# Keeping all sixteen pieces of image 0 on chip between its statistics and its first convolution

## The chip, the cores and the metric

The kernel runs on one core of a Trainium2 chip. The metric is device time in microseconds (us); lower is better. Engines are called PE (TensorE), DVE (VectorE), ACT (ScalarE), POOL (GpSimd) and SP (SyncE, which here only issues DMAs). Three runs of the kernel before gave a median of 11134.48 us (11132.05 to 11135.5).

## What is computed

The input x is four images of 192 channels and 128x128 pixels, f32. Two layers, both of the form x = x + conv(group_norm(x)):

```
x = x + L0(_gn(x))      # layer 0: 1x1 conv 192 -> 48 channels, split in three groups of 16:
                        #   x_0 : 1x1 conv
                        #   x_05: fractional Fourier transform in 2-D, magnitude and phase,
                        #         3x3 conv inside a window and 1x1 convs on them, transform back
                        #   x_1 : real 2-D FFT, 1x1 convs on magnitude and phase, inverse FFT
                        #   concatenate, 1x1 conv 48 -> 192
x = x + L1(_gn(x))      # layer 1: layer norm, projection, causal conv, selective scan over
                        #   16384 tokens with 384 channels x 16 states, gate, projection
_gn: 32 groups of 6 channels, mean and variance over a group's channels and all pixels
```

The change is in layer 0's group norm and its first 1x1 convolution, both of image 0. The group norm needs the mean and variance over the whole image before the first pixel can be convolved, so the image is read twice: once for the statistics, once for the convolution.

## The kernel before, in words

Layer 0 (`layer0`, L122) handles an image in sixteen pieces of 8 rows (1024 pixels); a piece is a tile of 96 partitions x 2 x 1024 f32, 768 KB, 8 KB of each partition. It has four generators for an image:

- `analysis` (L266): loads each piece (`load`, L196, a DMA issued by SP at L199), takes its statistics (`bn`, L202: four BATCH_NORM_STATS2 on DVE, L205), then combines them (L218, then the small matmuls L56 and L63 and the DVE steps L57 to L67 of `_group_stats`), scales the weights (L284), forms a bias (L287, L291) and convolves each piece: four matmuls (L301), one eviction with the bias on ACT (L305) into `x1`, and after each pair of pieces two DMAs of 192 KB, issued by ACT (L311), to the DRAM tensor `d1`. `x1` has two buffers (pool `l0f`), each for one pair.
- `forward` (L314): loads 32 of the 48 channels of `d1` as one image `img` (2 MB, L317 on SP), transforms (`spectrum`, matmuls L233 and L243, evictions L236 and L249 on ACT, L251 on DVE) and forms magnitude and phase (`_polar`, L70: eleven steps on DVE, a RECIPROCAL of 6.54 us among them, L84 to L96). This goes in three passes: two halves of the fractional transform, then the real FFT. Results go to DRAM (`dmag` and `dp` at L326, `dh` at L333). The pool `l0u` with seven buffers holds a pass.
- `backward` (L337): convolutions on magnitude and phase, and the transforms back.
- `synthesis` (L481): last convolution, added to x, written to `xmid`, and the statistics for layer 1.

The sixteen pieces' tiles come from the pool `l0x` of seven buffers, which `analysis` and `synthesis` of all images share. The last four pieces (KEEP = 4) stay on chip between the statistics and the convolution; the convolution takes these first and then the other twelve, which are loaded a second time from x.

`weave` (L520) calls the generators of up to four images in turn: first `analysis` of image 0 alone, then in step p `backward` of image p-1, `forward` of p, `analysis` of p+1 and `synthesis` of p-2. This sets the order in which the program is written. In layer 0 the compiler then orders the instructions of each engine itself, by its own estimate of when each is ready and by their place in the program, and adds the waits. The order on an engine or a DMA queue is fixed from then on: an instruction that waits holds up all behind it on its engine. Layer 1 (`layer1`, L593) has an order written out by hand, which the change doesn't touch; it takes over when layer 0's pools are closed, and its scans run from 1377 us to the end.

Of the kernel before, what the change touches and what calls it, by code (L numbers as in the profile page):

```python
# [33 lines left out]
NPIECE = S // ROWS  # L34
# [87 lines left out]
def layer0(tc, x, xmid, st2, w):  # L122

    nc = tc.nc
    B = x.shape[0]
    KEEP = 4
    LOADS = 14
    with ExitStack() as ctx, ExitStack() as inner:
        def pool(name, bufs, ctx=inner, **kw):
            return ctx.enter_context(tc.tile_pool(name=name, bufs=bufs, **kw))  # L130

        kp = pool("l0k", 1, ctx)
        dram = pool("l0d", B, ctx, space=DRAM)
        xp = pool("l0x", 7, ctx)
        sp = pool("l0s", 2, ctx)
        psB = pool("l0r", 2, ctx, space=PSUM)
        cp = pool("l0c", 1)
        fp = pool("l0f", 2)
        imp = pool("l0i", 2)
        zp = pool("l0z", 2)  # L140
        up = pool("l0u", 7)
        vp = pool("l0v", 4)
        qp = pool("l0q", 1)
        psA = pool("l0p", 4, space=PSUM)

        def const(name, cp=cp):
# [46 lines left out]
        def split(v):  # L193
            return v.rearrange("(t p) f -> p t f", p=CH)

        def load(b, p):  # L196
            xt = xp.tile([CH, 2, PIECE], F32, name="xt")
            src = x[b].rearrange("c h w -> c (h w)")[:, p * PIECE : (p + 1) * PIECE]
            nc.sync.dma_start(out=xt, in_=split(src))  # L199
            return xt  # L200

        def bn(st, p, xt):  # L202
            for t in range(2):
                for q in range(PIECE // 512):
                    nc.vector.bn_stats(  # L205
                        st[:, t, p * (PIECE // 512) + q, :], xt[:, t, q * 512 : (q + 1) * 512]
                    )
# [7 lines left out]
        def bn_done(st, out, psum):  # L215
            mv = sp.tile([CH, 2, 2], F32, name="mv")
            for t in range(2):
                nc.vector.bn_aggr(mv[:, t, :], st[:, t, :, :])  # L218
            _group_stats(nc, sp, psum, g_ones, mv, out, 1e-5)
# [43 lines left out]
            nc.tensor.matmul(ps[:, 0:n], bd[:, i, :], rhs, start=True, stop=True)  # L263
            return ps[:, 0:n]

        def analysis(b, got):  # L266


            st = sp.tile([CH, 2, NPIECE * (PIECE // 512), 6], F32, name="st")
            kept = {}  # L270
            for p in range(NPIECE):
                xt = load(b, p)
                if p >= NPIECE - KEEP:
                    kept[p] = xt
                bn(st, p, xt)
                yield
            gst = sp.tile([CH, 2, 2], F32, name="gst")
            bn_done(st, gst, in_a)

            w1r = fp.tile([CH, 2, 128], F32, name="w1r")
            for t in range(2):
                nc.vector.tensor_scalar(w1r[:, t, :], w1T[:, t, :], gst[:, t, 1:2], None, ALU.mult)  # L284
            ps = psA.tile([128, 512], F32, name="ps")
            for t in range(2):
                nc.tensor.matmul(  # L287
                    ps[:, 0:1], w1r[:, t, :], gst[:, t, 0:1], start=t == 0, stop=t == 1
                )
            b1 = fp.tile([128, 1], F32, name="b1")  # L290
            nc.vector.tensor_scalar(b1, ps[:, 0:1], -1.0, None, ALU.mult)  # L291
            d1 = got["d1"] = dram.tile([3 * NC, S * S], F32, name="d1")
            for p in (*range(NPIECE - KEEP, NPIECE), *range(NPIECE - KEEP)):
                xt = kept.pop(p, None) or load(b, p)
                if p % 2 == 0:
                    x1 = fp.tile([128, 2, 512], F32, name="x1")
                ps = psA.tile([128, 512], F32, name="ps")
                for t in range(2):
                    for q in range(2):
                        half = slice(64 * q, 64 * (q + 1))  # L300
                        nc.tensor.matmul(  # L301
                            ps[half], w1r[:, t, half], xt[:, t, q * 512 : (q + 1) * 512],
                            start=t == 0, stop=t == 1,
                        )
                nc.scalar.activation(x1[:, p % 2, :], ps, AF.Identity, bias=b1)  # L305
                if p % 2 == 1:
                    at = d1[:, (p - 1) * PIECE : (p + 1) * PIECE].rearrange(
                        "c (e q f) -> q c e f", e=2, q=2
                    )
                    for q in range(2):  # L310
                        nc.scalar.dma_start(out=at[q], in_=x1[64 * q : 64 * q + 3 * NC])  # L311
                yield
# [168 lines left out]
        def synthesis(b, got, early):  # L481
# [5 lines left out]
            def fetch(p):  # L487
                if p < NPIECE:
                    cat = cats[p % 2]
                    for q in range(2):  # L490
                        at = slice(p * PIECE + q * 512, p * PIECE + (q + 1) * 512)
                        nc.sync.dma_start(out=cat[64 * q : 64 * q + NC, :], in_=d1[0:NC, at])
                        nc.sync.dma_start(out=cat[64 * q + NC : 64 * q + 3 * NC, :], in_=dimg[:, at])
                if len(early) <= p + len(early) < NPIECE:
                    xts.append(load(b, p + len(early)))
# [24 lines left out]
        def weave(works, early=None):  # L520

            n = max(count for _, count in works)
            for i in range(n):
                for work, count in works:
                    for _ in range((i + 1) * count // n - i * count // n):
                        next(work, None)
                if early is not None and i == LOADS:
                    early.extend(load(B - 1, p) for p in range(KEEP))
            for work, _ in works:
                for _ in work:  # L530
                    pass

        got = [{} for _ in range(B)]
        weave([(analysis(0, got[0]), 1)])
        early = []
        for p in range(B + 1):
            works = []
            if p:  # L540
                works.append((backward(p - 1, got[p - 1]), 19))
            if p < B:
                works.append((forward(p, got[p]), 9))
            if p + 1 < B:
                works.append((analysis(p + 1, got[p + 1]), 2 * NPIECE + 1))
            if p >= 2:
                works.append((synthesis(p - 2, got[p - 2], []), NPIECE + 1))
            weave(works, early if p == B else None)
# [697 lines left out]
def program(tc, x, out, w):  # L1246
    B = x.shape[0]
    with (
        tc.tile_pool(name="keep", bufs=1) as keep,
        tc.tile_pool(name="mid", bufs=1, space=DRAM) as mid,  # L1250
    ):
        st2 = keep.tile([CH, B, 2, 2], F32, name="st2")
        xmid = [mid.tile([C, S * S], F32, name=f"xmid{b}") for b in range(B)]
        first = layer0(tc, x, xmid, st2, w)
        second = layer1(tc, xmid, [out[b].rearrange("c h w -> c (h w)") for b in range(B)], st2, w)
        next(first)
        next(second)
        ready = False
        for _ in first:
            for _ in range(2):  # L1260
                ready = ready or next(second)
        for _ in second:
            pass
# [16 lines left out]
```

## Time and profile before

| | before |
|---|---|
| median of three runs | 11134.48 us |
| the profiled execution's own time | 11134.09 us |
| its span, first to last instruction | 11132.3 us |
| loads of pieces in layer 0 (`xt<-in_x`, 768 KB each) | 176 |
| image 0: last statistics on a piece end | 68.4 us |
| image 0: first and last convolution eviction start | 79.65 and 118.53 us |
| `img` of image 0: load issued, first transform matmul | 127.52 and 137.76 us |
| image 1: statistics combined (L218) | 191.59 us |
| image 1: first and last matmul of its first convolution | 208.0 and 261.7 us |
| `img` of image 1, 2, 3: load issued | 269.80, 521.47, 795.92 us |
| layer 1's scans begin | 1377 us |

How to read it: times of instructions are in us from the span's start. A line of a timeline gives the start, the duration, the engine, the line of the code, the operation, the tiles (out<-in) and how many instructions were merged; in square brackets the idle time of the engine before it and what ended that. SPq and ACTq are the DMA queues that SP and ACT issue from. In a table of stretches, the columns give busy time (and number) of each engine, the granted TensorE clock as a share of full speed, the mean busy share of the 16 DMA engines and what they moved. The span and the execution's own time differ by 1.8 us, which lie around the span.

### The profile page before, as it was taken

The numbers are of one execution on the slowest core, as the hardware profiler recorded it, in microseconds if no ns is written. First come the engines' busy times: TensorE is split into PE (matmuls) and PEld (weight loads), VectorE is DVE, ScalarE is ACT, GpSimd is POOL, SyncE is SP. The second block draws the span as 40 slices with busy tenths as digits, with TensorE's granted clock in tenths as the row PEclk, the third lists the DMA queues.
The fourth block names the chain that finished last, engine by engine and source line by source line (L and its number), as shares of the span: only waits on it lengthen the run. The fifth ranks groups of instructions, "written<-read, shape, count | busy, mean of one in ns | idle before, by whom it ended". The sixth has DMA issues, their size and how long they took to land.

```text
span 11132.3 us, 168105 instructions
## 1 busy us (share of the span) xinstructions
PE 9935.4 (89%) x55026; PEld 6973.1 (63%) x55026; DVE 10209.6 (92%) x11587; ACT 9346.5 (84%) x19303; POOL 9523.9 (86%) x4342
## 2 busy tenths in 40 slices
PE   4777799999999999999999999999999999999998
PEld 2444366666666666666666666666666666666666
DVE  5666699999999999999999999999999999999999
ACT  2333299999999999999999999999999999999997
POOL 0000199999999999999999999999999999999999
PEclk8888799999999999999999999999999999999999
DMA  8786734434434434434334334344444334344343
GB/s 235 187 228 177 234 106 118 123 103 121 123 107 119 117 108 124 114 110 125 114 110 125 113 112 124 111 113 125 113 111 125 113 110 124 108 117 123 108 118 96
DMA packets 1357308, 1416.61 MB, mean 127 GB/s; under 512 B 920730, under 2 KB 972175, under 8 KB 1355791
## 3 DMA queue, kind: packets, MB, share of 16 engines
q1 hardware_dynamic: 1335950, 1342.94, 43.4%
q0 software_dynamic: 13312, 50.34, 1.4%
q10 hardware_dynamic: 7168, 12.59, 0.3%
q8 instruction: 436, 7.14, 0.3%
q14 instruction: 442, 3.61, 0.1%
HBM read 1230.12 MB, written 155.33 MB: 124 GB/s over the span
## 4 chain that ended last, share of the span: by engine, by line
PE 46%; ACT 23%; DVE 15%; issue 5%; DMA 2%; POOL 0%; SPq 0%; DVEq 0%; POOLq 0%; ACTq 0%
PE ps L1014 12%; PE ps L798 12%; DVE h L988 10%; ACT da L910 8%; PE op L974 7%; PE ps L1053 6%; ACT L695 4%; DVE op L931 3%; ACT op L910 3%; ACT dbT L959 2%; PE ps L951 1%; ACT L810 1%; ACT u L810 1%; PE ps L767 1%; DMA carry<-h 1%
## 5 line engine op out<-in xcount | busy, mean ns | idle before, releaser
L1001 POOL TENSOR_TENSOR hc<-h,c 128x1024 f32<-128x1024 f32 x3072 | 7220.9, 2369 | 326.3 <-DVE h L988 174.3
L988 DVE TENSOR_TENSOR_SCAN h<-da,carry,op 128x512 f32<-128x512 f32 x4464 | 5526.6, 1262 | 137.9 <-DMA carry<-h 134.5
L910 ACT ACTIVATE da<-dt,c_A_log 128x512 f32<-128x512 f32 x4608 | 3251.1, 737 | 239.6 <-DVE h L988 221.4
L1014 PE MATMUL ps<-ident,hc 128*128 128x128 f32 x24576 | 3315.0, 281 | 4.5 <-POOL hc L1001 4.5
L1014 PEld LDWEIGHTS ps<-ident,hc 128*128 128x128 f32 x24576 | 2943.8, 147 | 344.7 <-issue 312.5
L959 ACT ACTIVATE dbT<-ps,bT 128x128 f32<-128x128 f32 x8192 | 2274.6, 397 | 0.0
L798 PE MATMUL ps<-s,wc 128*128 128x512 f32 x4608 | 2129.8, 593 | 0.0
L974 PE MATMUL op<-ident,dbT 128*128 128x128 f32 x8192 | 1456.4, 300 | 628.8 <-ACT dbT L959 478.1
L988 DVE TENSOR_TENSOR_SCAN h<-op,carry,db 128x512 f32<-128x512 f32 x1488 | 1837.6, 1262 | 2.0 <-ACT da L910 1.1
L942 POOL TENSOR_TENSOR db<-dtu,b 128x1024 f32<-128x1024 f32 x768 | 1820.8, 2371 | 6.1 <-DVE nmr L641 6.1
L974 PEld LDWEIGHTS op<-ident,dbT 128*128 128x128 f32 x8192 | 1037.7, 149 | 1144.8 <-ACT dbT L959 534.8
L931 DVE TENSOR_TENSOR op<-ps,b 128x512 f32<-128x512 f32 x2560 | 1719.1, 672 | 3.9 <-ACT ps L891 3.9
L798 PEld LDWEIGHTS ps<-s,wc 128*128 128x128 f32 x4608 | 804.9, 190 | 682.8 <-issue 682.3
L910 ACT ACTIVATE op<-dt,c_A_log 128x512 f32<-128x512 f32 x1536 | 1084.2, 706 | 167.4 <-DVE h L988 166.5
L1053 PE MATMUL ps<-yg,c_woT 128*96 128x512 f32 x1536 | 702.7, 594 | 0.0
L695 ACT ACT_TABLE_LOAD x511 | 655.6, 1283 | 9.7 <-PEq L1270 0.7
L514 POOL DMA_DIRECT2D xmid<-xt x64 | 42.3, 661 | 569.9 <-DVE xt L510 542.6
L856 POOL TENSOR_TENSOR dtu<-dt,u 128x512 f32<-128x512 f32 x384 | 490.8, 1278 | 0.6 <-DMA cat<-dimg 0.6
L817 ACT ACTIVATE zs<-ps 128x512 f32<-128x512 f32 x384 | 229.4, 597 | 304.6 <-PE ps L805 304.6
L1053 PEld LDWEIGHTS ps<-yg,c_woT 128*96 128x96 f32 x1536 | 244.0, 163 | 338.4 <-issue 338.4
L205 DVE BATCH_NORM_STATS2 st<-xt 96x6 f32<-96x512 f32 x512 | 322.4, 677 | 100.5 <-DMA xt<-in_x 99.3
L78 POOL TENSOR_TENSOR u<-u 128x1024 f32<-128x1024 f32 (+1 forms) x12 | 29.7, 2477 | 447.6 <-ACT u L77 447.6
(173 smaller groups left out, 10018.9 us busy)
## 6 DMA issues: line engine op xcount, KB each, us to landing
c<-dbc SPq DMA_DIRECT2D x1024, 512.0 KB, 4.7
b<-dbc SPq DMA_DIRECT2D x768, 512.0 KB, 4.7
xt<-in_x SPq DMA_DIRECT2D x176, 768.0 KB, 8.3
xmid<-xt POOLq DMA_DIRECT2D x64, 768.0 KB, 6.3
xm<-xmid SPq DMA_DIRECT2D x128, 384.0 KB, 3.7
carry<-h SPq DMA_DIRECT2D x3072, 1.0 KB, 1.9
xr<-xmid SPq DMA_DIRECT2D x128, 384.0 KB, 6.1
out<-xr SPq DMA_DIRECT2D x128, 384.0 KB, 3.3
```

Source lines behind the costliest of these rows:

```text
L695: nc.scalar.preload_act_table_set("natural_log_exp_and_others")
L798: nc.tensor.matmul(g["c", j][0], wc[:, j, k, :], rhs, start=k == 0, stop=k == 5)
L856: nc.gpsimd.tensor_tensor(g["dtu", j], g["dt", j], g["u", j], ALU.mult)
L910: nc.scalar.activation(da, got[n]["dt", j], AF.Exp, scale=A[:, j, st : st + 1])
L931: nc.vector.tensor_tensor(dbs[s], g["dp", j][0], g["b", k % NG][:, q, :], ALU.mult)
L942: nc.gpsimd.tensor_tensor(db, _bc(g["dtu", j], 1, G), g["b", sg], ALU.mult)
L959: nc.scalar.activation(t[:, blk, :], g["tu", j][0][:, at], AF.Identity, scale=g["bT"][:, blk, st : st + 1],)
L974: nc.tensor.transpose(db[:, blk * 128 : (blk + 1) * 128], t[:, blk, :], ident)
L988: nc.vector.tensor_tensor_scan(h[:, q, :], das.pop(s), dbs.pop(s) if db is None else db[:, q, :], 0.0 if ch == 0 else g["before"][:, j, st ...
L1001: nc.gpsimd.tensor_tensor(hc, h, g["c", sg], ALU.mult)
L1014: nc.tensor.matmul(py[:, blk, :], hc[:, q, blk * 128 : (blk + 1) * 128], ident, start=first, stop=sg == NG - 1 and q == G - 1 and blk == N ...
L1053: nc.tensor.matmul(g["po", t][0][0:CH], woT[:, j, t * CH : (t + 1) * CH], g["yg", j], start=j == 0, stop=j == NJ - 1,)
```

## The change

For image 0 alone, `analysis` keeps all sixteen pieces. Pieces 0 to 8 go to a new pool `l0y` of nine buffers (72 KB of each partition), pieces 9 to 15 to the seven buffers of `l0x`. The convolution takes pieces 10 to 15 first, then 0 to 9, and loads none again. The new pool is closed as soon as this `analysis` has been written; the five pools `l0i`, `l0z`, `l0u`, `l0v` and `l0q` of the later steps (107,008 bytes of each partition by their tiles' sizes), which used to be opened at the start, are opened after it at the address at which the new pool stood. The other images keep KEEP = 4 and load twelve pieces again.

```diff
     KEEP = 4
+    XBUFS = 7
     LOADS = 14
...
-        xp = pool("l0x", 7, ctx)
+        xp = pool("l0x", XBUFS, ctx)
...
         fp = pool("l0f", 2)
-        imp = pool("l0i", 2)
-        zp = pool("l0z", 2)
-        up = pool("l0u", 7)
-        vp = pool("l0v", 4)
-        qp = pool("l0q", 1)
         psA = pool("l0p", 4, space=PSUM)
...
-        def load(b, p):
+        def load(b, p, xp=xp):
...
-        def analysis(b, got):
+        def analysis(b, got, more=None):
...
             kept = {}
+            keep = NPIECE if more else KEEP
             for p in range(NPIECE):
-                xt = load(b, p)
-                if p >= NPIECE - KEEP:
+                xt = load(b, p, more if more and p < NPIECE - XBUFS else xp)
+                if p >= NPIECE - keep:
                     kept[p] = xt
...
-            for p in (*range(NPIECE - KEEP, NPIECE), *range(NPIECE - KEEP)):
+            last = NPIECE - (XBUFS // 2 * 2 if more else KEEP)
+            for p in (*range(last, NPIECE), *range(last)):
                 xt = kept.pop(p, None) or load(b, p)
...
         got = [{} for _ in range(B)]
-        weave([(analysis(0, got[0]), 1)])
+        with tc.tile_pool(name="l0y", bufs=NPIECE - XBUFS) as more:
+            weave([(analysis(0, got[0], more), 1)])
+        imp = pool("l0i", 2)
+        zp = pool("l0z", 2)
+        up = pool("l0u", 7)
+        vp = pool("l0v", 4)
+        qp = pool("l0q", 1)
         early = []
```

## The prediction

> **What bounds the kernel now.** I read the page's slices first, to see where the change can act at all.
>
> ```profile
> ## 2 busy tenths in 40 slices
> PE   4777799999999999999999999999999999999998
> PEld 2444366666666666666666666666666666666666
> DVE  5666699999999999999999999999999999999999
> ```
>
> A slice is 278 us. Layer 0 fills the first five, and no engine is full there; from the sixth on layer 1's scans keep DVE, PE and POOL full. The table of stretches gives the same in numbers.
>
> ```profile
> 270.00:1377.00 1107.00, 820.98 (x2952) 451.19 (x2952) 722.47 (x905) 323.58 (x461) 95.91 (x111) 0.84 0.77 208
> 1377.00:11132.00 9755.00, 8988.85 (x51589) 6460.64 (x51588) 9348.12 (x10476) 8963.65 (x18762) 9420.66 (x4224) 0.96 0.41 115
> ```
>
> The columns are PE, PE's weight loads, DVE, ACT, POOL, clock, DMA share, GB/s. From 270 to 1377 us PE is busy 74%, DVE 65%, DMA 77%: layer 0 is bound by chains of waits in fixed orders, not by an engine. Layer 1's 9755 us are DVE at 96% and are not touched. So a gain can only be a layer 0 that ends earlier. The chain of waits that ended last breaks off at 898 us, so it says nothing on the start; I read timelines there. SP:
>
> ```profile
> 79.64 39.16 SPq L199 DMA_DIRECT2D xt<-in_x  x13
> 127.52 0.81 SPq L317 DMA_DIRECT2D img<-d  x1
> 128.39 8.08 SPq L199 DMA_DIRECT2D xt<-in_x  x7
> ```
>
> 32 loads of pieces stand ahead of img: 16 for image 0's statistics, 12 reloads, 4 of image 1. Three reloads were issued before 79.64; the 13 seen here are nine reloads and four loads of image 1. ACT, which evicts the convolution:
>
> ```profile
> 107.85 1.27 ACT L305 ACTIVATE x<-ps,b 128x512 f32<-128x512 f32 x2 [6.20 <-DMA d<-x]
> ...
> 118.53 1.27 ACT L305 ACTIVATE x<-ps,b 128x512 f32<-128x512 f32 x2 [6.79 <-DMA d<-x]
> ```
>
> It waits 25.3 us in all, six times, for the write of d1 that holds its x1 buffer, while PE's own waits for a reload are 4.6 us. The image's convolution is paced by writes that share the DMA engines with loads (0.99 busy from 82 to 127.5 us), not by the reloads' arrival as such. Then image 1, on DVE and PE:
>
> ```profile
> 116.57 2.47 DVE L205 BATCH_NORM_STATS2 st<-xt 96x6 f32<-96x512 f32 x4 [40.37 <-DMA xt<-in_x]
> ```
>
> ```profile
> 193.62 0.45 PE L56 MATMUL ps<-mv,c_g_ones 96*96 96x2 f32 x2 [30.38 <-DVE mv L218]
> 203.19 0.45 PE L63 MATMUL ps<-gs_d,c_g_ones 96*96 96x2 f32 x2 [9.11 <-DVE gs_d L61]
> 207.52 0.56 PE L287 MATMUL ps<-gst,w1r 96*128 96x1 f32 x2 [3.88 <-DVE w1r L284]
> ```
>
> ```profile
> 137.70:191.60 53.90, 24.37 (x96) 20.02 (x96) 48.19 (x65) 19.36 (x25) 4.71 (x2) 0.72 0.96 235
> ```
>
> DVE is idle 40 us for want of image 1's pieces, then from 137.7 to 191.6 it is 89% busy, because 12 pieces' statistics (48 instructions, 29.7 us) fall between the polar steps of forward of image 0. PE stands 43.4 us at the head of its queue for image 1's statistics. This is where the time is.
>
> **What the Trainium skill says.** "DMA: Bandwidth & Descriptors", section "Issuing engines are not separate DMA queues": DMAs from ACT and SP run on the same 16 engines and interleave. The trace agrees: a 192 KB write of d1 beside loads lands after 7.9 us (median). The same page, "Anatomy of one DMA — SWDGE (gpsimd) path": a wait happens on the issuing sequencer before dispatch, so it holds all behind it; SP's L326 waited 20.4 us for ACT with eight loads of pieces behind it. "TensorE: Matmul & The Clock Gate", Part 1: PE idles down to half clock after some microseconds; the trace grants 0.50 from 110 to 140 us, where PE waits. No page prices the reuse of a closed pool's memory.
>
> **The change part by part.** Sum against the profiled execution, 11134.1 us (span 11132.3, 1.8 around it; the median is 0.4 higher).
>
> 1. *First sixteen loads.* They need no freed buffer now. Statistics start every 3.155 us (24.88 to 65.90 us in 13 gaps) of which DVE works 2.47: DMA sets the pace with 1.02 to 1.04 busy, and goes on doing so. Worth 0. Pool boundaries issue nothing.
>
> 2. *Twelve reloads go*: 12 x 3.155 = 37.9 us of DMA time. Three ran by 75 us, when DMA would now be idle: worth 0. Nine, 28.4 us, lay in the full stretch. Image 1's loads take their place: from 79.6 us they get the buffers of pieces 10 to 15 as PE frees them, where before the buffers of 12 to 15 let reloads in. So about 13 of image 1's pieces instead of 4 have landed by 127 us. This rests on a load taking whichever buffer is free; the trace can't show that (rival below).
>
> 3. *img of image 0.* Its convolution has as many loads beside it as before, so its writes wait about as long: 0. Bounds: with nothing beside, PE's pace of 1.715 us a piece gives the last eviction at 82.75 + 14 x 1.715 + 0.7 = 107.5 and the write at 113 to 115, so 13 us gained; with image 1's last three loads also ahead of img, 3 x 3.155 = 9.5 lost. Since the loads no longer hold the convolution back, SP's order may put fewer ahead: I take 4 gained. The new wait, that img and the l0u tiles lie where pieces 0 to 8 were, costs 0: those matmuls end before the last write of d1, for which L317 waits anyway with the same loads queued behind it on SP. If that cover were gone, the price would be at most the 8 us from the last eviction to L317's issue.
>
> 4. *Statistics of nine pieces move* from between the polar steps into DVE's idle 40 us: 9 x 2.47 = 22.2 us. As DVE is 89% busy there and a pass waits for the buffers of the pass before, I take all 22 as forward's gain. Bounds: 0, if ACT or the u buffers pace it, and 42, as follows. Image 1's last three pieces land by 137.7 + 9.5 = 147, statistics combined at 151.5 against 193.5 (42 earlier). From there to the first matmul takes 5.2 us in image 0 and 16.4 in image 1, where a 6.54 us RECIPROCAL stood in between; with 16 again the convolution begins at 166 instead of 208 and its 54 us no longer lie across forward's third pass (216 to 262 us). PE's 43 us wait is not counted again: behind it stood only that convolution and a pass that had no buffers yet.
>
> 5. *Later.* The first stage ends when forward of image 0 does (last dh store issued at 296 us): 22 + 4 = 26 earlier, while img of image 1 has 42. From there all later work depends on these two, and no engine is full, so the 26 carry to 1377 us, and layer 1 starts 26 earlier.
>
> 11134.1 - 26 = **11108 us**.
>
> **The rivals.**
> - *The full lead carries*: image 1's convolution being out of the way is worth 42: 11092. For it: the third pass took 81 us between dp and dh stores (215 to 296) where the second took 33. Against: polar chains remain.
> - *Buffers in turn*: image 1's first load takes piece 9's buffer, convolved last. Then loads start at 107.5, four go ahead of img (107.5 + 2 + 12.6 = 122, plus 2.1 MB at 247 GB/s = 8.5: 130.6), img gains 7 and the other 12 loads fall among the polar steps as before: 11127. For it: nothing in the trace excludes it.
> - *Gain eaten*: one wait of the 16 us kind moves in a later order, as the compiler orders all of layer 0 anew (SP stood 16.0 and 24.0 us at single L492): 11124.
> - *Slower*: PE's order. With image 1's statistics early, the compiler may set image 1's L56 and its whole convolution ahead of forward's first L233. PE then begins forward at 157 + 46 (image 0's convolution took 73.5 to 119.8) = 203 instead of 137.8, 65 late, gets back the 22 and some 20 of the third pass: 11157. It decides once forward starts after 137.8 + 42 = 180 us. For it: PE already stood 30 us at that L56. Against: forward comes first in the program.
> - *The change does nothing*: excluded, as all sixteen pieces are kept and none can be loaded again.
>
> **How the numbers follow.** Forecast 0.31, full lead 0.19, gain eaten 0.20, buffers in turn 0.15, slower 0.15. A measurement of this kernel tells about 0.2%, 22 us, from no change. The first two lie beyond it: faster 0.50; the next two within: same 0.35; slower 0.15. Range: the full lead and one such 16 us wait less, 11076; upward no change and one such wait more, 11150, which leaves out most of the slower case. The forecast's own range is 11098 to 11112.
>
> **What would show it.** 164 loads of pieces instead of 176. DVE's statistics of image 1 starting near 85 us, not 116.6, and 13 of its pieces done by 130. L317 near 123. L218 of image 1 near 150; PE's wait at its L56 gone. The last dh store near 270, scans from about 1351. Wrong would be: image 1's first statistics after 105 (in turn); L301 of image 1 ahead of the first L233 (slower); the last dh store early but scans at 1377 (eaten).

## The result and the profile after

| | before | after |
|---|---|---|
| median of 15 runs each | 11134.22 us (11113.35 to 11148.74) | 11111.36 us (11102.22 to 11141.45) |
| ratio, 95% interval | | 0.9981 (0.9973 to 0.9989) |
| the profiled execution's own time, and its span | 11134.09, 11132.3 us | 11107.0, 11104.8 us |

The change gains 0.19%, about 21 us (12 to 30). The one profiled execution of each shows 27 us. The forecast was 11108 us, 26 less than before.

Lines of the code shift a little in the kernel after: the load of a piece is L195 (was L199), the statistics L201 and L214 (L205, L218), the scaled weights and the bias L281, L284 and L288 (L284, L287, L291), the convolution L299 and its eviction L303 (L301, L305), the writes of `d1` L309 (L311), the load of `img` L315 (L317), the stores of `dmag` and `dp` L324 (L326), of `dh` L331 (L333).

The page's slices and its list of DMA issues first. 176 loads of pieces have become 164, 12 x 768 KB less. Of the slices shown before, PE's first (4 before) and DVE's first four (5666) differ: the same work stands a little earlier.

```profile
PE   5777799999999999999999999999999999999998
DVE  6567699999999999999999999999999999999999
```

```profile
xt<-in_x SPq DMA_DIRECT2D x164, 768.0 KB, 8.5
```

SP's timeline shows what stands in the places of the reloads. 29 loads stand ahead of the first `img`, sixteen of image 0 and thirteen of image 1, and none is a reload. `img` is issued at 124.23 us (before 127.52), and image 1's at 240.67 (before 269.80).

```profile
76.99 37.42 SPq L195 DMA_DIRECT2D xt<-in_x  x13
124.23 0.82 SPq L315 DMA_DIRECT2D img<-d  x1
125.10 8.15 SPq L195 DMA_DIRECT2D xt<-in_x  x6
...
240.67 0.70 SPq L315 DMA_DIRECT2D img<-d  x1
241.43 5.38 SPq L331 DMA_DIRECT2D dh<-u  x1
...
270.33 0.39 SPq L331 DMA_DIRECT2D dh<-u  x1
```

DVE's timeline: image 1's statistics begin at 82.59 us (before 116.57). Thirteen pieces are done by 126.3, in what was an idle stretch of 40 us, and the statistics are combined (L214) at 147.63 (before 191.59).

```profile
82.59 2.47 DVE L201 BATCH_NORM_STATS2 st<-xt 96x6 f32<-96x512 f32 x4 [9.04 <-DMA xt<-in_x]
...
123.87 2.47 DVE L201 BATCH_NORM_STATS2 st<-xt 96x6 f32<-96x512 f32 x4 [0.32 <-DMA xt<-in_x]
...
147.63 1.88 DVE L214 BATCH_NORM_AGGREGATE mv<-st 96x2 f32<-96x192 f32 x2
```

PE's timeline: the 30 us wait at the first L56 of image 1 is gone. The two matmuls that follow it still wait for DVE, and image 1's convolution begins at 173.73 us (before 208.0).

```profile
154.44 0.25 PE L56 MATMUL ps<-mv,c_g_ones 96*96 96x2 f32 x2
...
168.98 0.48 PE L63 MATMUL ps<-gs_d,c_g_ones 96*96 96x2 f32 x2 [7.40 <-DVE gs_d L61]
173.24 0.56 PE L284 MATMUL ps<-gst,w1r 96*128 96x1 f32 x2 [3.79 <-DVE w1r L281]
173.73 1.97 PE L299 MATMUL ps<-xt,w1r 96*64 96x512 f32 x2
```

The table of stretches, with the columns used before (PE, weight loads, DVE, ACT, POOL, clock, DMA share, GB/s). In the first stretch PE is busy 39.2 us instead of 24.4, and the DMA engines only 59% instead of 96%, since thirteen of image 1's pieces have been loaded by then, instead of four. The rest of layer 0 and layer 1 look as before: the last two stretches have the same busy shares as the ones shown of the kernel before, only earlier.

```profile
137.70:191.60 53.90, 39.18 (x158) 25.21 (x158) 41.64 (x45) 23.54 (x32) 4.69 (x2) 0.84 0.59 150
```

```profile
270.00:1350.00 1080.00, 802.89 (x2879) 437.33 (x2878) 698.20 (x880) 309.24 (x431) 93.55 (x111) 0.82 0.77 208
1350.00:11104.00 9754.00, 8982.39 (x51600) 6455.73 (x51598) 9351.29 (x10478) 8959.74 (x18780) 9417.02 (x4224) 0.96 0.41 115
```

Followed along the program, the lead over before is 25.7 us at the last `dh` store of image 0, 29.1 at `img` of image 1, 21.8 at the store of `dimg`, with which backward of image 0 ends, 23.0 and 23.6 at `img` of images 2 and 3, and 21.5 where layer 1's scans begin (by the first scan instruction on DVE, 1357.24 instead of 1378.74). From there to the end the two executions take 9747.6 and 9753.6 us, with the same instructions in the same order. So four fifths of what is gained by 296 us are still there at the end, and the 6 us between 21 and 27 belong to layer 1 of these two executions, not to the change.

The order of each engine's instructions, compared between the two kernels, differs only at the start: PE's 55,026 instructions within the first 240, SP's DMAs within the first 120, DVE's instructions within the first 316, ACT's within the first 83, and POOL's nowhere.

### The profile page after: what moved, and what is told of

It is laid out like the page before. It is cut to its first block, busy times and chain, and to the rows that moved or that the text cites. A ratio compares the mean times of both kernels' runs of the same rounds, so it can differ in the third digit from the quotient of the medians.

```text
span 11104.8 us, 168074 instructions
## 1 busy us (share of the span) xinstructions
PE 9929.2 (89%) x55026; PEld 6968.1 (63%) x55026; DVE 10213.5 (92%) x11587; ACT 9336.4 (84%) x19303; POOL 9517.9 (86%) x4342
## 4 chain that ended last, share of the span: by engine, by line
PE 46%; ACT 24%; DVE 15%; issue 5%; DMA 2%; SPq 0%; POOL 0%; DVEq 0%; POOLq 0%; ACTq 0%
PE ps L1018 12%; PE ps L802 12%; DVE h L992 10%; ACT da L914 8%; PE op L978 7%; PE ps L1057 6%; ACT L699 4%; DVE op L935 3%; ACT op L914 3%; ACT dbT L963 3%; PE ps L955 1%; ACT L814 1%; ACT u L814 1%; DMA carry<-h 1%; PE ps L771 1%
## 5 line engine op out<-in xcount | busy, mean ns | idle before, releaser
L1033 PE MATMUL ps<-ddp,u 128*128 128x128 f32 x3072 | 405.9, 275 | 0.0
L201 DVE BATCH_NORM_STATS2 st<-xt 96x6 f32<-96x512 f32 x512 | 322.3, 677 | 83.5 <-DMA xt<-in_x 82.4
```

## The experiments

**The theories.** *DVE theory* (the prediction's step 4): the gain comes from nine pieces' statistics that no longer stand among forward's polar steps. *Lead theory* (the prediction's "full lead", in part): it comes from image 1's convolution, which runs 34 us earlier and so no longer lies across forward's third pass. *Reload theory*: image 0's convolution no longer waits for its data, and `img` comes earlier. *Address theory*: the pools that are opened later lie elsewhere or are laid out differently, and that moves the time.

Two quantities were read to tell them apart, the beginning of image 1's convolution and the lengths of forward's passes. The lengths come from SP's timeline of each run and are free of shifts of the start. The first two passes last from the issue of `img` of image 0 to its second `dp` store, the third from there to the last `dh` store.

| | image 1: convolution begins | first two passes | third pass | ratio to before, 95% interval |
|---|---|---|---|---|
| before | 208.0 us | 87.5 us | 81.0 us | 1 |
| e1, only the pools later | 206.9 us | 89.9 | 85.3 | 0.9995 (0.9987 to 1.0003) |
| e2, twelve loads that nothing reads | 211.9 | 94.1 | 80.9 | 1.0006 (0.9999 to 1.0012) |
| e5, before with fewer statistics | 200.3 | 80.4 | 83.2 | 0.9991 (0.9985 to 0.9998) |
| e6, convolution held back | 205.8 | 78.0 | 75.2 | 0.9989 (0.9983 to 0.9996) |
| after | 173.7 | 77.9 | 68.2 | 0.9981 (0.9973 to 0.9989) |
| after, once more | 174.1 | 77.5 | 65.6 | 0.9976 (0.9967 to 0.9985) |
| e3, pieces convolved in order | 183.1 | 85.7 | 69.6 | 0.9978 (0.9970 to 0.9987) |
| e4, four buffers of x1 | 168.1 | 78.4 | 64.9 | 0.9966 (0.9953 to 0.9978) |
| e7, image's chain of statistics first | 164.7 | 82.2 | 53.4 | 0.9957 (0.9944 to 0.9969) |
| e8, e4 and e7 together | 156.9 | 87.4 | 42.1 | 0.9930 (0.9916 to 0.9943) |
| e9, before with the chain first | 206.7 | 88.4 | 83.0 | 0.9987 (0.9980 to 0.9994) |

The runs were made on several chips, where the kernel before had medians of 11134 to 11155 us; each ratio is to the kernel before on the same chip.

The traces show besides what the end of the first stage hangs on. As soon as image 1's convolution is through, PE turns to backward of image 0 (`magQ`, then L373). DVE's first steps of that backward wait for L373, and the polar steps of forward's third pass stand behind them in DVE's order. First the kernel before, then the one after:

```profile
262.26 1.12 PE L263 MATMUL ps<-magQ,c_bd 128*128 128x512 f32 x2
268.87 0.59 DVE L385 SCALAR_TENSOR_TENSOR s<-ps,c_bdb,c_rowmask 128x360 f32<-128x360 f32 x1 [2.71 <-PE ps L373]
273.24 1.22 DVE L84 TENSOR_TENSOR u<-u 128x1040 f32<-128x1040 f32 x1
```

```profile
234.44 1.12 PE L259 MATMUL ps<-magQ,c_bd 128*128 128x512 f32 x2
241.05 0.59 DVE L383 SCALAR_TENSOR_TENSOR s<-ps,c_bdb,c_rowmask 128x360 f32<-128x360 f32 x1 [0.86 <-PE ps L371]
243.79 1.22 DVE L84 TENSOR_TENSOR u<-u 128x1040 f32<-128x1040 f32 x1
```

From that turn of PE to the last `dh` store of image 0 it takes 33.7 us in before, e1, e2, e5, e9 and the second profile of after, 34.0 in e4, 35.9 in after, 36.4 to 39.8 in e3, e7 and e8, and only in e6 less, 26.2. So in all of these but e6 the first stage ends a nearly fixed time after image 1's convolution does.

### Only the pools opened later

The kernel before, with the five pools opened after the first `analysis`; no piece is kept longer.

```diff
-        imp = pool("l0i", 2)
-        zp = pool("l0z", 2)
-        up = pool("l0u", 7)
-        vp = pool("l0v", 4)
-        qp = pool("l0q", 1)
...
         weave([(analysis(0, got[0]), 1)])
+        imp = pool("l0i", 2)
+        zp = pool("l0z", 2)
+        up = pool("l0u", 7)
+        vp = pool("l0v", 4)
+        qp = pool("l0q", 1)
```

> The kernel before with one part of the change alone: the five pools of the later steps are opened after image 0's analysis; nothing more is kept, the twelve reloads stay. The theory (image 1's loads move forward by the reloads' DMA time, and with them its statistics and convolution leave forward's way) expects no change, 11134 within 5 us, img of image 0 issued at 127 to 128. The rival that the gain comes from the order or the place of things, by chance of the compiler, expects some of the 23 us here.

Measured: 0.9995 (0.9987 to 1.0003), no difference. The order on all five engines is that of the kernel before, so its profile also shows what chance does within one order: `img` was issued at 124.04 us (before 127.52), the passes took 89.9 and 85.3 us (before 87.5 and 81.0). A difference of 3 us at one place in one execution says nothing. The address theory finds no support: opening the pools later changes neither the order nor, clear of noise, the time.

### The loads kept, the gain of keeping taken away

The kernel after, which loads twelve pieces of image 0 a second time into buffers that nothing reads. It leaves nothing out.

```diff
                 xt = kept.pop(p, None) or load(b, p)
+                if more and p < NPIECE - KEEP:
+                    load(b, p)
```

> The changed kernel, all sixteen pieces kept, but with twelve pieces of image 0 loaded once more all the same into the buffers of l0x, read by nothing. The theory expects the gain gone to within 6 us of before (11128 to 11140): image 1's first statistics near 116 instead of 82.6. The rival, that image 0's convolution gains because it no longer waits for data, expects the gain kept: 11105 to 11118.

Measured: 1.0006 (0.9999 to 1.0012): with the loads back the whole gain is gone, although the convolution takes its data from on-chip tiles as in the kernel after. DVE's timeline shows image 1's first statistics, and SP's the loads ahead of `img`:

```profile
124.16 2.47 DVE L201 BATCH_NORM_STATS2 st<-xt 96x6 f32<-96x512 f32 x4 [49.27 <-DMA xt<-in_x]
```

```profile
78.32 39.02 SPq L195 DMA_DIRECT2D xt<-in_x  x15
124.81 0.81 SPq L317 DMA_DIRECT2D img<-d  x1
```

The statistics wait 49 us for their first piece, which comes 8 us later than in the kernel before, and are combined at 195.5 us. `img` is issued where the kernel after issues it. So what counts of the twelve loads is the place they take from image 1's pieces: DMA time, and buffers of `l0x`, which this run does not tell apart (the DMA engines are busy all the time from 82 to 127 us in it, by 1.03 of their time). That image 0's convolution finds its data on chip is worth nothing by itself. The reload theory falls.

### Nine pieces' statistics left out

The kernel before, with the statistics of image 1 taken from seven pieces. Loads and convolutions are all there; the values of the statistics differ.

```diff
-                bn(st, p, xt)
+                if b != 1 or p < 4 or p > 12:
+                    bn(st, p if b != 1 or p < 4 else p - 9, xt)
...
-            bn_done(st, gst, in_a)
+            bn_done(st[:, :, 0:14, :] if b == 1 else st, gst, in_a)
```

> The kernel before, without the statistics of nine of image 1's sixteen pieces (4 to 12): these are loaded, but their 36 statistics instructions are left out, 22.2 us of DVE. It prices step 4's DVE part alone, since image 1's last pieces, and so its combined statistics, come as late as before. The prediction's step expects 22 us less, 11112. The theory as the traces now suggest it (DVE's part of the lead was only about 10 us, the rest came from image 1's convolution leaving the third pass) expects 6 to 12 us less, 11122 to 11128, with the second dp store at 203 to 208 instead of 215.

Measured: 0.9991 (0.9985 to 0.9998), 10 us (2 to 17), where the DVE theory wanted 22. The stretch from 137.7 to 191.6 us of this run shows why:

```profile
137.70:191.60 53.90, 24.76 (x98) 20.08 (x98) 33.65 (x37) 20.24 (x25) 5.08 (x2) 0.72 0.98 246
```

DVE does 14.5 us less here than in the kernel before (48.19), but PE not more (24.76 to 24.37) and ACT hardly more. PE still waits 21.7 us at its first L56 of image 1:

```profile
185.88 0.45 PE L56 MATMUL ps<-mv,c_g_ones 96*96 96x2 f32 x2 [21.68 <-DVE mv L218]
```

The first two passes become 7.1 us shorter than before (9.5 than in e1), and the third no shorter.

The run does not show DVE's part alone, though, as it was meant to. Without those statistics image 1's are combined 6.8 us earlier, its convolution begins 7.7 us earlier, PE is through with it 5.5 us earlier (256.78 us, before 262.26), and the last `dh` store comes 5.5 us earlier too. What this execution gains up to there is the convolution's lead. Where layer 1's scans begin, nothing of it is left in the profile (1379.60 us, in e1 1379.85), while the times say 10 us; that was not settled. What falls is that these statistics are worth 22 us.

### Image 1's convolution held back

The kernel after, with image 1's scale made to depend on a tile of the second half's phases (times 0, so that no value changes). Its statistics are as early as after the change; its convolution can't begin before forward's second pass is nearly done.

```diff
+            if b == 1:
+                for _ in range(3):
+                    yield
             bn_done(st, gst, in_a)
+            if b == 1:
+                hold = fp.tile([CH, 1], F32, name="hold", bufs=1)
+                nc.vector.tensor_scalar(hold, held[0][0:CH, 0:1], 0.0, None, ALU.mult)
+                for t in range(2):
+                    nc.vector.tensor_add(gst[:, t, 1:2], gst[:, t, 1:2], hold)
...
+        held = []
...
+                if b == 0 and half == 1:
+                    held.append(pha)
```

> The changed kernel, with image 1's convolution held back: its scaled weights wait for the end of the second polar pass of image 0 (two tiny DVE additions of a zero worked out from that pass's phase). Its statistics stay early. If image 1's early convolution is worth some 13 us through the third pass, the last dh store slips from 270 to 283 or later, img of image 1 from 241 to about 268, and the time is 11120 to 11128. If DVE's statistics were the whole of it, the time stays at 11111 within 5 us.

Measured: 0.9989 (0.9983 to 0.9996), 12 us (4 to 19) instead of 21 to 27. PE begins the convolution at 205.8 us, with the wait moved to L292 (the bias, L284 after the change):

```profile
205.31 0.59 PE L292 MATMUL ps<-gst,w1r 96*128 96x1 f32 x2 [29.39 <-DVE w1r L289]
205.83 1.97 PE L307 MATMUL ps<-xt,w1r 96*64 96x512 f32 x2
```

SP's timeline of the same run:

```profile
254.10 0.39 SPq L343 DMA_DIRECT2D dh<-u  x1
...
271.46 0.71 SPq L325 DMA_DIRECT2D img<-d  x1
...
279.78 0.39 SPq L343 DMA_DIRECT2D dh<-u  x1
```

The first two passes keep what the change gave them (78.0 us), the third loses 7 to 10 us of it (75.2 against 68.2 and 65.6), and `img` of image 1 is back where it was before the change (271.5; 269.8 before). By the times about half of the gain is lost with the early convolution, but the intervals of e6 and after overlap. What is left can't be put down to the early statistics, because the edit also moved the order. The first transforms of the third pass now stand ahead of the held convolution on PE, where in the kernel after they begin behind its start (182.94 us):

```profile
157.99 1.03 PE L229 MATMUL ps<-c_rf,img 128*128 128x256 f32 x4
```

The convolution itself takes 47.7 us here (54.2 before), and behind its end only 26.2 us follow to the last `dh` store. This execution leads the one before by 16.2 us at that store and by 1.4 where the scans begin. So e5 and e6 do not split the gain between the statistics and the convolution. They show that the nine pieces' statistics are not worth 22 us, and that with the convolution held back `img` of image 1 gains nothing.

### The kernel after once more, on another chip

Run beside e3, e4 and e7, so that these can be compared on one chip.

> The changed kernel once more, unaltered, as the yardstick for the three beside it on the same chip: 0.9975 to 0.9987 of the kernel before (it was 0.9981).

Measured: 0.9976 (0.9967 to 0.9985), in agreement with the first measurement.

### The pieces convolved in the order of their loads

```diff
-            last = NPIECE - (XBUFS // 2 * 2 if more else KEEP)
+            last = 0 if more else NPIECE - KEEP
```

Pieces 0 to 8 lie in the new pool, so the buffers that image 1 can have come free only with piece 9.

> The changed kernel with the pieces of image 0 convolved in the order 0 to 15 instead of 10 to 15, 0 to 9: the buffers of l0x come free last, so image 1's first load can start only some 15 us later, as in the prediction's rival of buffers in turn, while the writes of d1 have the DMA engines to themselves. The theory (image 1's lead counts through DVE and the third pass, img's through forward's start, and the stage ends with the later of the two) expects img of image 0 issued at 110 to 117 instead of 124, image 1's statistics combined 5 to 15 us later than 148, and in sum no gain over the changed kernel: within 8 us of it. The rival that img's start alone counts expects 8 to 12 us less than the changed kernel.

Measured: 0.9978 (0.9970 to 0.9987), the same as after. But the way is another. SP's timeline:

```profile
94.66 16.21 SPq L195 DMA_DIRECT2D xt<-in_x  x8
119.00 0.82 SPq L315 DMA_DIRECT2D img<-d  x1
```

Eight instead of thirteen loads go between the first eviction and `img`, which comes 5 us earlier. In return image 1's statistics are combined at 175.9 us, 28 later, and PE waits for them again (22.4 us at L56). The chain from there to the first convolved piece takes 7.2 us, because only two short polar steps and no RECIPROCAL stand before its end on DVE. The expectation had the directions and the sum, but neither size: `img` was to come at 110 to 117 us (119.0), the statistics 5 to 15 us later (28). By the time, the order in which the change convolves the pieces is therefore not what makes it work. In this one profile 15.6 us of lead over before are left where the scans begin, 21.5 and 22.0 in the two of after.

### Four buffers for x1

Image 0's evictions get four buffers instead of two, in the new pool.

```diff
-                    x1 = fp.tile([128, 2, 512], F32, name="x1")
+                    x1 = more.tile([128, 2, 512], F32, name="x1", bufs=4) if more else fp.tile([128, 2, 512], F32, name="x1")
```

> The changed kernel with four x1 buffers instead of two for image 0 (in the new pool), which takes away ACT's waits for writes of d1 (17.7 us in the changed kernel). By the prediction's bound for img the convolution would run at PE's pace and img be issued up to 10 us earlier, at 114 to 120. The theory expects a part of that at the end, 3 to 8 us less than the changed kernel, as image 1's loads do not come earlier with it.

Measured: 0.9966 (0.9953 to 0.9978), beside 0.9976 for the kernel after on that chip. ACT no longer waits for writes of `d1` between 75 and 140 us (17.7 us in four waits after the change, 23.0 in six in its second profile), and `img` is issued at 117.2 us, 7 earlier. The intervals of the two ratios overlap, so that this is faster is likely rather than shown. In the profile the last `dh` store comes 10 us earlier than after the change (260.5 us), and the scans begin 1 to 2 us earlier (1355.5). In the kernel after, two of these waits look like this on ACT:

```profile
109.84 1.26 ACT L303 ACTIVATE x<-ps,b 128x512 f32<-128x512 f32 x2 [5.10 <-DMA d<-x]
114.15 1.26 ACT L303 ACTIVATE x<-ps,b 128x512 f32<-128x512 f32 x2 [3.05 <-DMA d<-x]
```

### The chain of statistics ahead of the polar steps

After the change, image 1's statistics wait 26 us on their way into the convolution (147.6 to 173.7 us). DVE's timeline shows where: L59, of 0.09 us, stands in DVE's order behind four polar steps and a RECIPROCAL, the last of which alone takes 6.55 us. "VectorE: DVE Perf Modes" of the Trainium skill ("First, the fixed hardware budget") says of it that it divides iteratively, with eight repeats, and gives no time; here it takes 5.4 times as long as a TENSOR_TENSOR of the same tile (1.22 us).

```profile
154.74 0.15 DVE L57 TENSOR_SCALAR gst<-ps 96x2 f32<-96x2 f32 x1 [4.68 <-PE ps L56]
...
159.65 6.55 DVE L87 RECIPROCAL u<-u 128x1024 f32<-128x1024 f32 x1
166.12 0.09 DVE L59 TENSOR_TENSOR gs_d<-mv,gst 96x2 f32<-96x2 f32 x1
```

The edit gives this chain priority where the compiler orders the instructions; it holds for all four images.

```diff
+            with tc.high_priority():
-            gst = sp.tile([CH, 2, 2], F32, name="gst")
-            bn_done(st, gst, in_a)
+                gst = sp.tile([CH, 2, 2], F32, name="gst")
+                bn_done(st, gst, in_a)
...
-            b1 = fp.tile([128, 1], F32, name="b1")
-            nc.vector.tensor_scalar(b1, ps[:, 0:1], -1.0, None, ALU.mult)
+                b1 = fp.tile([128, 1], F32, name="b1")
+                nc.vector.tensor_scalar(b1, ps[:, 0:1], -1.0, None, ALU.mult)
```

> The changed kernel with a higher priority, for all images, for the small steps between the combined statistics and the first convolution (L56 to L288), so that the compiler sets them ahead of polar steps on DVE. In the changed kernel they took 26 us for image 1 (147.6 to 173.7), with a RECIPROCAL of 6.55 us in between. The theory expects that stretch to fall to 8 to 15 us, img of image 1 to be issued 8 to 16 us earlier than 240.7, and the time to fall by 3 to 10 us. If only forward's passes set the end of the stage, it stays within 3 us of the changed kernel.

Measured: 0.9957 (0.9944 to 0.9969), about 48 us faster than before and 21 than after; the interval and that of the kernel after on that chip have only 0.9967 to 0.9969 in common. The expectation was 3 to 10 us less than after; the five runs give twice its upper end. The profile shows 9 us of lead over the kernel after where the scans begin (1347.8 us); more than that can only lie in layer 1, which the edit doesn't touch and whose length differs between single executions (9731 us in e7's profile, 9748 and 9765 in the two of after), so the 21 are probably too many. On DVE the scaled weights are ready before the RECIPROCAL begins:

```profile
154.26 0.16 DVE L57 TENSOR_SCALAR gst<-ps 96x2 f32<-96x2 f32 x1 [3.08 <-PE ps L56]
...
159.10 0.47 DVE L282 TENSOR_SCALAR w1r<-c_w1T,gst 96x128 f32<-96x128 f32 x2
...
162.13 6.54 DVE L87 RECIPROCAL u<-u 128x1024 f32<-128x1024 f32 x1
```

The convolution begins 9 us earlier (164.65), the first two passes pay 4 for it (82.2), and the third takes 53.4 us instead of 66 to 68.

### Both together

> The changed kernel with both of the last two edits that helped: four x1 buffers for image 0 and the higher priority of the small statistics steps. If img of image 0 coming earlier (7 us in the run with four buffers) and image 1's convolution coming earlier (some 9 us) add up, it is 0.9935 to 0.9957 of the kernel before; if the stage's end is set by one of them alone, it stays at 0.9957 or above.

The kernel after with the edits of e4 and e7. Measured: 0.9930 (0.9916 to 0.9943), about 78 us faster than before and past the expected 0.9935, with a median of 11064.17 us the fastest kernel of this study. PE goes through the chain without one long wait, and the convolution begins at 156.9 us:

```profile
149.89 0.30 PE L56 MATMUL ps<-mv,c_g_ones 96*96 96x2 f32 x2 [1.76 <-DVE mv L214]
...
151.11 0.30 PE L63 MATMUL ps<-gs_d,c_g_ones 96*96 96x2 f32 x2
...
156.90 3.65 PE L300 MATMUL ps<-xt,w1r 96*64 96x512 f32 x16
```

The gains of e4 and e7 over the kernel after, 0.10% and 0.19%, add up to 0.9947 with it; the measured ratio lies 0.17% below that. The intervals are about that wide, so part of it may be chance. In the profile the lead over before is 47.7 us at the last `dh` store and 57.3 where the scans begin; where the ten between them are gained, and the rest up to 78, was not settled.

### The chain of statistics first, in the kernel before

The edit of e7 alone, without the kept pieces.

> The kernel before with that higher priority alone, nothing more kept. There the small steps of image 1 took 16.4 us (191.6 to 208.0) with a RECIPROCAL in between. If the priority works by itself, image 1's convolution starts some 7 to 10 us earlier and the time falls by 4 to 12 us (0.9989 to 0.9996); if it needs image 1's pieces to be early, it stays within 3 us of before.

Measured: 0.9987 (0.9980 to 0.9994), 15 us faster than before, but not in the way that was expected. Image 1's convolution begins at 206.7 us, 1.3 earlier, because L61 lands behind a RECIPROCAL all the same:

```profile
195.12 6.54 DVE L87 RECIPROCAL u<-u 128x1024 f32<-128x1024 f32 x1
201.59 0.09 DVE L61 TENSOR_TENSOR gs_d<-gs_d,mv 96x2 f32<-96x2 f32 x1
```

At the last `dh` store of image 0 nothing is gained (296.6 us, before 296.0). The lead appears with the later images: 9.0 us at `img` of image 3, 12.0 where the scans begin. In e7 and e8 image 1's statistics are combined before the first polar step of image 0, in e9 between the two halves; that priority needs the former to help image 1 is likely from these runs and was not tested by itself.

## Why the prediction was right, step by step

The time, the sign and the size came out: 26 us were forecast, 21 (12 to 30) were measured, and the place (image 0's first stage) and the carry to the end are as forecast. Its largest term was not: the sum came out by luck, because what that term stood for is not what ended the stage, and the lead that did end it stood only among the bounds and rivals.

1. *First sixteen loads, 0.* Held within what the profile can tell: image 0's statistics are combined at 65.65 us after and 68.29 before, but at 66.27 in e1, which has the order of before. That is chance.

2. *Twelve reloads' DMA time goes to image 1.* Held, and to the piece: thirteen pieces loaded ahead of `img`, their statistics done by 126.3 us. A load takes whichever buffer is free; the rival "buffers in turn" put the first statistics after 105 us, and they came at 82.6. e2 shows that this term carries the whole effect.

3. *`img` of image 0, 4 gained; memory take-over, 0.* The profile shows 3.3, but e1 shows 3.5 without the change, so no gain is shown and the term is nearer 0. The take-over cost nothing: L315 waited 9.5 us after the change, and for the writes of `d1` alone.

4. *Nine pieces' statistics, 22.* This is the step that failed. It took DVE, 89% busy, as forward's pace, and did not count PE's 43 us at image 1's statistics, since behind that wait "stood only that convolution and a pass that had no buffers yet". Taking the statistics away gave 10 us (2 to 17), and image 1's convolution moved with them. And what stood behind the wait is what ended the stage: in PE's order the third pass's transforms lie inside that convolution, after the change they ran from 182.9 us, ahead of the second `dp` store (202.2), and the last `dh` store follows the convolution's end by 33.7 us before and 35.9 after.

   Along this chain the numbers add up. Image 1's statistics are combined 44.0 us earlier (42 were foreseen). Their way into the convolution takes 26.1 us instead of 16.4 (the prediction kept 16), because PE came to L56 behind L239 (4.7 us of DVE's wait) and a RECIPROCAL and polar steps followed: 9.7 lost. The convolution takes 60.7 instead of 54.2, now beside two passes; whether that is why was not tested: 6.5 lost. Another 2.2 go behind its end, where DVE waits 3.7 us for a piece of image 2. That leaves the 25.7 us at the last `dh` store. The prediction named this mechanism as a rival with a weight of 0.19 and priced it at 42; it was this rival with three losses, and that they brought it to the forecast's 22 + 4 was luck.

5. *The 26 carry whole.* 25.7 at the last `dh` store, 21.5 where the scans begin: four fifths of it. Image 1's 29 us of lead at its `img` shrinks to 23 at the next image.

The slower rival, PE set behind image 1's statistics and convolution, did not come about: the first transform matmul stood ahead of them as before. "Gain eaten" had the compiler order all of layer 0 anew. Only the first 316 instructions of an engine changed at most, so no later order was new; the 4 us between 25.7 and 21.5 were lost within the old one.

One reading of the prediction was too simple. It puts the clock of 0.50 from 110 to 140 us down to PE's waiting, but from 110 to 115 us PE is busy for 4.85 of 5 us at that clock, and its waits just ahead were of 1.3 to 1.9 us.

## What to carry to other kernels

A load that is saved is worth what the next transfer in its place lets begin earlier; follow that one (here the next image's statistics, then its convolution) instead of the consumer of the load that is gone. A busy share of 89% in a stretch between waits doesn't make the engine its pace. To leave the work out is a cheap trial, but look what else has moved with it before you put the gain down to that work. Before a wait is left out of a sum, look at what stands behind it in that engine's order, and what ends the stage. When data come earlier, look at the short steps that hand them on: on an engine with a fixed order each can stand behind the longest instruction of other work, and to order them first gave 9 us more here in the profiles and 21 by the times.

## What the runs showed of the hardware that was not expected

- Two executions with the same order of instructions on every engine (before and e1), on two chips, differ by 2 to 4 us at single places in the first 300 us, while the times of the kernels agree within 0.05%.
- Two `x1` buffers, each for a pair of 128x512 evictions, were too few where the 192 KB writes share the DMA engines with 768 KB loads: ACT waited 17.7 to 25.3 us in all for them in four to six waits, and not at all with four.
- With the chain of statistics ordered first and four such buffers, the granted TensorE clock from 137.7 to 191.6 us is 0.97, after the change 0.84 and before it 0.72, as PE's busy time there goes from 24.4 to 39.2 to 49.3 us. "TensorE: Matmul & The Clock Gate" of the Trainium skill, Part 1, lets the clock fall where PE idles; these three stretches agree.
